# A macaron block with tree FFNs: pacing the scatters by the work beside them, and spreading the gathers of f's attention over its query steps

## The chip, the cores and the metric

The kernel runs on one core of a Trainium2 chip. Times are device microseconds (us) of that core, medians of several executions. One execution of the kernel before was also recorded by the profiler; its page and its trace are what is read here. The engines are PE (TensorE: matmuls; PEld its weight loads), DVE (VectorE), ACT (ScalarE), POOL (GpSimd) and SP (SyncE, which here only issues transfers).

## The reference

The input x has four sequences of 1024 tokens of 256 numbers, f32. Three parts are applied in turn:

```
x = x + 0.5 * ffn1(layernorm(x))
x = x + attention(layernorm(x))      # 16 heads, low-rank keys and values, rotary embedding, paged and causal
x = x + 0.5 * ffn2(layernorm(x))
```

The two ffn have the same weights. Each normalises its input to xn and then computes

```
q = tree_q(xn); k = tree_k(xn); v = tree_v(xn)         # relu
att = softmax(q k^T / sqrt(256)) v                      # within a sequence, 1024 x 1024, one head
y = xn + att
result = y + tree_f(y)                                  # gelu
```

A tree is a hard-routed feed-forward layer: each token walks down 8 levels of a binary tree, taking a side by the sign of a dot product at each node, and ends in one of 256 leaves. Each leaf is a small network of its own, 256 to 16 to 256, with biases b1 and b2.

## The kernel before, in words

**Tiles.** The 4096 tokens are 32 token tiles of 128 (NT), eight per sequence (TPB). Routing goes in groups of four tiles (GT). Leaves are taken in 32 blocks of 8, since 8 leaves of width 16 fill 128 columns. Tokens are sorted by block in DRAM, each block's share padded to whole tiles of 128 rows; there are at most 63 such leaf tiles.

**One tree.** `route` (called in groups by `routes`) transposes four tiles of xn, multiplies them with all nodes' weights (L320), compares (L328), and turns the bits into a one-hot block number per token (`oh`, L353) and running counts (`acc`, L355). `place` (L446) makes from the counts the first row of each block, and in `ranks` (L400 to L420), twice for 16 tiles each, the row (the *slot*) of each token: a 128x16 sum `sf` in f32, cast to int32 into `slot_*`. `scatter` (L529) then lets POOL issue one indirect transfer for each token tile (L531), which writes the 128 rows of that tile to their slots in DRAM (`xs`, for f `xs_f`). `leaves` (L620) loops over the leaf tiles in pipelined steps: SP loads `xg` (L629), PE transposes it (L635), DVE copies it to `xgT` (L637), PE multiplies with the block's first weights (L653, L656), DVE masks (`hm`, L661), PE transposes (L671), ACT applies the nonlinearity (L673), PE multiplies with the second weights (L678), ACT copies the result (L680) and SP writes it to DRAM, `os_q`, `os_k`, `os_v`. For f, DVE also casts each row's token number (`tok`, L666) and POOL scatters the result to token order (`ytok`, L682).

**Order within a tree FFN.** Route and place q; scatter q; route k, in whose group steps (`before(k)`) q's first weights are transposed (`load_first`, from pieces `raw_q`); q's leaves, with `place` for k running beside them, one piece per leaf tile (`with_steps`); scatter k; build k's weights and route v; k's leaves beside place for v; scatter v; build v's weights; v's leaves. During v's leaves, `coming` gathers keys and queries of the first sequence and keys of the second.

SP issues the loads ahead of this in an order that the scheduler sets: pieces of the first weights (`raw_q` and so on, L555), biases (`b_q`, L562, which `split_b1`, L568 to L575, splits into bf16 terms on DVE), second weights (`w_q`, L545) and, in the first FFN, zeros for `xs` and the sorted results (L250).

**Gathers.** `fetch` (L712) lets POOL gather a token tile's rows of q, k or v out of the sorted results (`y_q`, `y_k`, `y_v`), `fetch_b2` (L726) gathers the second biases (`b_q`, `b_k`, and for v straight into the value tile `vb`). `turned` (L933) adds the two on DVE (L938), transposes on PE (L943) and copies on ACT into `qT` or `kT` (L944); `value` (L925) adds on DVE (L931). Each of these tags has three buffers.

**The attention of q, k and v.** It is ordered by hand for PE, DVE, ACT and POOL (`in_order`): what the program writes first goes first on each engine. There are 32 steps s, one for each query tile; a sequence is also called a batch, 0 to 3. In a step `begin_weights` transposes an older tile's weights `pr` (L763) and copies them (`pT`, L764; half on DVE, half on ACT); `score` multiplies (L740), takes the maximum (`mx`, L748), scales it, and lets ACT take the exponential (L753); the older tile is then weighed with the values (L768) and `xn` updated (L770). In step 3 two more tiles are weighed. A dictionary `plan` holds what else is done: `at(step, where, do, ...)`, with where 0 (ahead of the step's scores), 1 (after the scores are issued and their maximum) or 2 (at the step's end). By the plan `begin(t)` issues the gathers of tile t's value, query and (for sequences 2 and 3) key, `add(t)` adds them, `turn(t)` does the rest. Further entries: `number` writes token numbers into xn's last column and clears `xs_f`; `begin_settling` and `settled` gather f's second bias (`b_f`) and add it and y to the residual (L1017, two adds for each tile); `place_run` places tokens for f in three runs of 24, 4 and 4 tiles (RUNS, `in_runs`), `scatter_run` scatters a run. f's routing of the last sequences lies in the same steps. The last four tiles are placed and scattered behind the attention, between pieces of the building of f's weights.

**Queues.** Transfers of SP are issued in SP's order; indirect ones in POOL's. Zeros for `xs_f` and the second weights of k, v and f go through ACT's queue. Outside the parts ordered by hand a scheduler orders the instructions; `keep_in_program_order` pins one among its like.

Of the kernel before, what the change touches and what calls it, by code (L numbers as in the profile page):

```python
# [71 lines left out]
def macaron_kernel(ctx: ExitStack, tc: tile.TileContext, a: dict, out: bass.AP):  # L72
# [327 lines left out]
    def ranks(pool, oh, acc, slot, lo, hi, first, skips=()):  # L400
# [17 lines left out]
        for part, t0 in slot:  # L418
            if t0 == lo:
                nc.vector.tensor_copy(part, sf)  # L420
# [25 lines left out]
    def place(pool, oh, acc, slot, gblk, sel):  # L446
# [6 lines left out]
        for h in range(2):  # L453
            ranks(pool, oh, acc, slot, h * NT // 2, (h + 1) * NT // 2, first)
            yield
# [8 lines left out]
    def in_runs(pool, oh, acc, slot, gblk, sel):  # L464
# [9 lines left out]
        def run(k):  # L474
# [25 lines left out]
            for t in range(lo, hi, NT // 2):  # L500
                ranks(pool, oh, acc, slot, t, min(t + NT // 2, hi), firsts[0], skips)
                yield
# [21 lines left out]
    def slot_of(slot, t):  # L524
        for part, t0 in slot:
            if t0 <= t < t0 + part.shape[1]:
                return part[:, t - t0 : t - t0 + 1]

    def scatter(f, slot, views, lo=0, hi=NT):  # L529
        for t in range(lo, hi):  # L530
            nc.gpsimd.indirect_dma_start(  # L531
                out=views[t],
                out_offset=bass.IndirectOffsetOnAxis(ap=slot_of(slot, t), axis=0),
# [4 lines left out]
    def views_of(f):  # L538
        return dram_disjoint_views(xs[f], NT)
# [168 lines left out]
    def fetch(pool, f, t, slot, bufs=3, tag=None):  # L708
# [7 lines left out]
            in_offset=bass.IndirectOffsetOnAxis(ap=slot_of(slot, t), axis=0),  # L716
# [55 lines left out]
    def ffn(first: bool, last: bool):  # L772
# [13 lines left out]
        with ExitStack() as es:  # L786
# [3 lines left out]
            for nm in FFFS:  # L790
                lows = (0, NT // 2, *RUNS[1:]) if nm == "f" else (0, NT // 2, NT)
                slot.append(
                    [
                        (idx.tile([P, hi - lo], I32, name=f"slot_{nm}{lo}"), lo)
                        for lo, hi in zip(lows, lows[1:])
                    ]
                )
# [21 lines left out]
            with ExitStack() as ws, banks(0, 8):  # L819
# [8 lines left out]
                with ExitStack() as hs, ExitStack() as rs:  # L828
                    raw = stage(rs, "raw", 1, "right")
                    pp = stage(hs, "place", 1)  # L830
                    with ExitStack() as rt:
# [43 lines left out]
                        drain(place(pp, *hot, slot[0], gblk[0], sel[0]))  # L875
                        scatter(0, slot[0], views_of(0))
                        hot = hots_of(pp, 1, 2)
                        routes(hp, 1, *hot, leaf[1], lambda k: drain(islice(build, 3 * (k > 0))))
                        drain(build)
# [5 lines left out]
                        with_steps(leaves(*what), place(pp, *hot, slot[1], gblk[1], sel[1]))  # L885
                        scatter(1, slot[1], views_of(1))
# [87 lines left out]
            with in_order(), qs, ExitStack() as ats, banks(2, 4):  # L974
# [18 lines left out]
                def begin(t):  # L993
# [8 lines left out]
                    for g in (now[0], *now):  # L1002
                        next(g)
# [569 lines left out]
```

## Time and profile before

| what | us |
|---|---|
| median of 13 executions | 2766.95 (2760.96 to 2775.38) |
| the profiled execution | 2759.72 |
| its span, first to last instruction | 2757.9 |
| PE busy | 2462.3 |
| DVE busy | 1522.4 |
| ACT busy | 1068.6 |
| POOL busy | 866.8 |

The profiled execution lies 7.2 us below the median, and 1.8 us of it lie outside the span. The mean clock granted to TensorE is 0.953 of full speed. The page shows busy times of the engines, the span in 40 slices, the chain that ended last and the costliest groups of instructions. Further views come from the trace: a timeline (start, duration, engine, line, operation, out<-in, and in brackets the idle time ahead and what ended it), a table of waits (engine, what it was about to do <- what it waited for: total, times, longest), and a table of windows (duration, then busy time and count for each engine, granted clock PEclk, share of the transfer engines, GB/s). L numbers are lines of the kernel before.

### The profile page before, as it was taken

The page shows a single profiled execution, that of the slowest core. Times are in us where ns is not written, and L with a number is a line of the kernel's source. Part 1 is how long each engine was busy: PE and PEld are TensorE (multiplying, and loading weights), DVE is VectorE, ACT ScalarE, POOL GpSimd, SP SyncE. Part 2 cuts the span into 40 slices and gives each one's busy share as a digit, 9 for nine tenths or more (in the row PEclk, how much of TensorE's full clock was granted, in tenths as well). Part 3 has the DMA queues.
Part 4 walks back from the last instruction along what each step waited for, and adds up shares of the span by engine and source line. Part 5 has one row for each costly group of instructions (what it writes and reads, how often), then busy time and mean ns, then how long its engine had stood idle before and what let it go on. Part 6 is the DMA issues. An engine that isn't in the chain of part 4 may idle for free. (4 is left out here: it accounts for less than half of the span.)

```text
span 2757.9 us, 42663 instructions
## 1 busy us (share of the span) xinstructions
PE 2462.3 (89%) x14352; PEld 1485.2 (54%) x14390; DVE 1522.4 (55%) x4105; ACT 1068.6 (39%) x2491; POOL 866.8 (31%) x978
## 2 busy tenths in 40 slices
PE   7879889899987699999999999989899899999774
PEld 3556567566665444444344344345666675666553
DVE  7654545344566566666666567556545454445643
ACT  3424334222324325555555545534343342332431
POOL 0440425356454421101101100004404255664453
PEclk9989989999998889999999999999999899999997
DMA  9965667373226400000000000005746675531455
GB/s 271 322 203 167 207 213 222 117 198 88 67 87 191 143 1 1 1 1 1 1 1 1 1 1 2 1 33 171 220 159 204 212 228 157 160 88 57 156 143 159
DMA packets 236693, 321.20 MB, mean 116 GB/s; under 512 B 28305, under 2 KB 207778, under 8 KB 232360
## 3 DMA queue, kind: packets, MB, share of 16 engines
q1 hardware_dynamic: 150480, 170.24, 20.6%
q0 software_dynamic: 38640, 100.90, 11.7%
q10 hardware_dynamic: 47336, 47.06, 5.7%
q8 instruction: 129, 2.11, 0.3%
q14 instruction: 108, 0.88, 0.1%
HBM read 193.59 MB, written 129.33 MB: 117 GB/s over the span
## 5 line engine op out<-in xcount | busy, mean ns | idle before, releaser
L1344 DVE TENSOR_REDUCE mxh<-big 128x1 f32<-128x512 f32 (+3 forms) x768 | 392.8, 551 | 220.3 <-PE big L1337 218.2
L1378 ACT ACTIVATE pTh<-big 128x512 f32<-128x512 f32 (+3 forms) x768 | 336.7, 491 | 331.9 <-PE big L1337 295.8
L1337 PE MATMUL big<-kTh,qTh 32*128 32x512 f32 (+3 forms) x1536 | 410.8, 536 | 3.2 <-ACT kTh L1319 1.6
L1371 PE MATMUL big<-qTh,kTh 32*128 32x512 f32 (+3 forms) x1536 | 351.9, 529 | 0.0
L661 DVE SCALAR_TENSOR_TENSOR hm<-eid,xg,sm 128x128 f32<-128x128 f32 x399 | 138.1, 346 | 300.7 <-PE sm L656 296.4
L673 ACT ACTIVATE hid<-sm 128x128 f32<-128x128 f32 x399 | 110.8, 278 | 425.3 <-PE sm L671 423.7
L740 PE MATMUL two<-kT,qT 128*128 128x512 f32 x512 | 236.2, 606 | 10.1 <-ACT pr L753 5.2
L768 PE MATMUL sm<-vb,pT 128*128 128x256 f32 x1024 | 234.4, 382 | 11.1 <-DVE pT L764 11.1
L320 PE MATMUL sm<-xT,nwT 128*128 128x512 f32 (+2 forms) x528 | 240.4, 599 | 2.8 <-ACT xT L314 2.8
L768 PEld LDWEIGHTS sm<-vb,pT 128*128 128x128 f32 x1024 | 191.6, 191 | 44.6 <-issue 13.4
L635 PE MATMUL sm<-ident,xg 128*128 128x128 f32 x798 | 164.6, 290 | 37.7 <-DMA xg<-xs_f 21.8
L1371 PEld LDWEIGHTS big<-qTh,kTh 32*128 32x128 f32 x1536 | 117.6, 183 | 149.2 <-DVE mxh L1344 75.8
L637 DVE COPY xgT<-sm 128x256 f32<-128x256 f32 x399 | 166.2, 416 | 27.5 <-PE sm L635 24.1
L1337 PEld LDWEIGHTS big<-kTh,qTh 32*128 32x128 f32 x1536 | 152.1, 183 | 46.0 <-ACT pTh L1378 27.4
L680 ACT COPY og<-sm 128x256 f32<-128x256 f32 x399 | 148.6, 373 | 60.5 <-PE sm L678 17.0
L1389 PE MATMUL sm<-pTh,vpad 128*32 128x512 f32 (+3 forms) x1536 | 166.7, 498 | 4.7 <-ACT pTh L1378 4.7
L328 DVE TENSOR_SCALAR bits<-sm,thr 128x512 bf16<-128x512 f32 (+1 forms) x132 | 96.5, 732 | 122.2 <-PE sm L320 121.6
L320 PEld LDWEIGHTS sm<-xT,nwT 128*128 128x128 f32 x528 | 98.5, 196 | 108.2 <-issue 89.8
L740 PEld LDWEIGHTS two<-kT,qT 128*128 128x128 f32 x512 | 94.8, 195 | 109.3 <-issue 100.9
L314 ACT COPY xT<-sm 128x512 f32<-128x512 f32 (+1 forms) x130 | 69.5, 582 | 190.4 <-PE sm L311 190.3
L531 POOL DMA_INDIRECT xs<-xn,slot_v x64 | 63.5, 993 | 240.6 <-DVE slot_v L420 221.7
L531 POOL DMA_INDIRECT xs<-xn,slot_q x64 | 61.8, 966 | 214.9 <-DVE slot_q L420 196.0
(295 smaller groups left out, 4413.2 us busy)
## 6 DMA issues: line engine op xcount, KB each, us to landing
xg<-xs SPq DMA_DIRECT2D x298, 128.5 KB
xs_f<-zero ACTq DMA_DIRECT2D x2, 8127.0 KB
xs<-zero SPq DMA_DIRECT2D x2, 8095.5 KB
xg<-xs_f SPq DMA_DIRECT2D x101, 129.0 KB
os_q<-og SPq DMA_DIRECT2D x101, 128.0 KB
os_v<-og SPq DMA_DIRECT2D x101, 128.0 KB
os_k<-og SPq DMA_DIRECT2D x96, 128.0 KB
raw_q<-in_q_w SPq DMA_DIRECT2D x8, 1024.0 KB
```

Source lines behind the costliest of these rows:

```text
L320: nc.tensor.matmul(pl, nwT[:, c, f, r * P : (r + 1) * P], xT[:, c, :], start=(c == 0), stop=(c == KC - 1),)
L635: nc.tensor.transpose(pa[:, c, :], xg[:, x0 + c * P : x0 + (c + 1) * P], ident)
L637: nc.vector.tensor_copy(xT, pa)
L661: nc.vector.scalar_tensor_tensor(hm, eid, xg[:, lf : lf + 1], ph, ALU.is_equal, ALU.mult)
L680: nc.scalar.copy(og, po)
L740: nc.tensor.matmul(ps[:, n0 : n0 + 512], qT[:, c, i * P : (i + 1) * P], kT[:, c, n0 : n0 + 512], start=(c == 0), stop=(c == KC - 1),)
L768: nc.tensor.matmul(po, pT[:, j, :], vb[:, j, :], start=(j == 0), stop=(j == TPB - 1))
L1337: nc.tensor.matmul(ps[:, :n], qT[r : r + HPAD, hg, i * P : (i + 1) * P], kT[r : r + HPAD, hg, n0 : n0 + n], start=True, stop=True,)
L1344: nc.vector.tensor_reduce(maxima(b, hg)[:, i, c, u : u + 1], ps[:, :n], AX.X, ALU.max)
L1371: nc.tensor.matmul(ps[:, off:], kT[r : r + HPAD, hg, j * P : (j + 1) * P], qT[r : r + HPAD, hg, qb * QN + off : (qb + 1) * QN], start=True ...
L1378: nc.scalar.activation(pT[:, u, off:], ps[:, off:], AF.Exp, scale=1.0 / math.sqrt(HD))
L1389: nc.tensor.matmul(acc[r : r + HPAD, off:], vpads[b % 2][:, j, 4 * hg + 2 * pair + u, :], pTs[pair][:, u, off:], start=(j == 0), stop=(j = ...
```

## The change

Four things are changed.

- `ranks` no longer casts its slots; it hands the f32 columns out in a list `rows`. Each scatter of a token tile has its own cast of one column (128x1) on DVE directly ahead of its transfer. `slot_*` is one tile per tree.
- q's scatter, 32 transfers in a row before, runs beside k's routing, five tiles for each of its group steps. k's and v's scatters run beside the leaf tiles, one token tile for each, behind the pieces of `place`. f's first run is scattered in nine places of steps 27 to 29, two or three tiles each.
- In the attention stage the gathers for q are begun for tile t at step t-6, added and turned at t-5; those of v and k of sequences 2 and 3 one tile per step. For the values of sequence 1 there are lists of steps. Settling for f takes one tile per step from step 9 on.
- `xs_f` is cleared by eight transfers in steps 6 to 20 in place of one in step 5.

```diff
...
-    def ranks(pool, oh, acc, slot, lo, hi, first, skips=()):
+    def ranks(pool, oh, acc, rows, lo, hi, first, skips=()):
...
         nc.vector.tensor_reduce(sf, row, AX.X, ALU.add)
-        for part, t0 in slot:
-            if t0 == lo:
-                nc.vector.tensor_copy(part, sf)
+        rows += [sf[:, k : k + 1] for k in range(n)]
...
-    def place(pool, oh, acc, slot, gblk, sel):
+    def place(pool, oh, acc, rows, gblk, sel):
...
         for h in range(2):
-            ranks(pool, oh, acc, slot, h * NT // 2, (h + 1) * NT // 2, first)
+            ranks(pool, oh, acc, rows, h * NT // 2, (h + 1) * NT // 2, first)
...
-    def in_runs(pool, oh, acc, slot, gblk, sel):
+    def in_runs(pool, oh, acc, rows, gblk, sel):
...
             for t in range(lo, hi, NT // 2):
-                ranks(pool, oh, acc, slot, t, min(t + NT // 2, hi), firsts[0], skips)
+                ranks(pool, oh, acc, rows, t, min(t + NT // 2, hi), firsts[0], skips)
...
-    def slot_of(slot, t):
-        for part, t0 in slot:
-            if t0 <= t < t0 + part.shape[1]:
-                return part[:, t - t0 : t - t0 + 1]
...
-    def scatter(f, slot, views, lo=0, hi=NT):
-        for t in range(lo, hi):
+    def scatter(f, slot, rows, views, *ts, pinned=True):
...
+        for t in ts:
+            cast = nc.vector.tensor_copy(slot[:, t : t + 1], rows[t])
+            if pinned:
+                tc.keep_in_program_order(cast)
...
                 out=views[t],
-                out_offset=bass.IndirectOffsetOnAxis(ap=slot_of(slot, t), axis=0),
+                out_offset=bass.IndirectOffsetOnAxis(ap=slot[:, t : t + 1], axis=0),
...
-    def views_of(f):
-        return dram_disjoint_views(xs[f], NT)
+    def scattering(f, slot, rows, n):
...
+        views = dram_disjoint_views(xs[f], NT)
+        for t in range(0, NT, n):
+            scatter(f, slot, rows, views, *range(t, min(t + n, NT)))
+            yield
...
             in_=osrt[f],
-            in_offset=bass.IndirectOffsetOnAxis(ap=slot_of(slot, t), axis=0),
+            in_offset=bass.IndirectOffsetOnAxis(ap=slot[:, t : t + 1], axis=0),
...
             for nm in FFFS:
-                lows = (0, NT // 2, *RUNS[1:]) if nm == "f" else (0, NT // 2, NT)
-                slot.append(
-                    [
-                        (idx.tile([P, hi - lo], I32, name=f"slot_{nm}{lo}"), lo)
-                        for lo, hi in zip(lows, lows[1:])
-                    ]
-                )
+                slot.append(idx.tile([P, NT], I32, name=f"slot_{nm}"))
...
                         build = load_first(raw, 0, w1, ahead)
-                        drain(place(pp, *hot, slot[0], gblk[0], sel[0]))
-                        scatter(0, slot[0], views_of(0))
+                        rows = []
+                        drain(place(pp, *hot, rows, gblk[0], sel[0]))
+                        going = scattering(0, slot[0], rows, 5)
                         hot = hots_of(pp, 1, 2)
-                        routes(hp, 1, *hot, leaf[1], lambda k: drain(islice(build, 3 * (k > 0))))
-                        drain(build)
...
+                        def beside(k):
+                            drain(islice(build, 3 * (k > 0)), islice(going, 1))
...
+                        routes(hp, 1, *hot, leaf[1], beside)
+                        drain(build, going)
...
                         b1, ahead = load_raw(raw, 1)
-                        with_steps(leaves(*what), place(pp, *hot, slot[1], gblk[1], sel[1]))
-                        scatter(1, slot[1], views_of(1))
+                        rows = []
+                        with_steps(
+                            leaves(*what),
+                            place(pp, *hot, rows, gblk[1], sel[1]),
+                            scattering(1, slot[1], rows, 1),
+                        )
...
                     ahead += [load_part(raw2, 2, *p) for p in PART[2:]]
-                    with_steps(leaves(*what), place(pp, *hot, slot[2], gblk[2], sel[2]))
-                    scatter(2, slot[2], views_of(2))
+                    rows = []
+                    with_steps(
+                        leaves(*what),
+                        place(pp, *hot, rows, gblk[2], sel[2]),
+                        scattering(2, slot[2], rows, 1),
+                    )
...
                 vbs.append(ap.tile([P, TPB, E], F32, name="vb1", bufs=1))
-                views = views_of(3)
-                placing = in_runs(pf, *hot_f, slot[3], gblk[3], sel[3])
+                views = dram_disjoint_views(xs[3], NT)
+                rows_f = []
+                placing = in_runs(pf, *hot_f, rows_f, gblk[3], sel[3])
...
-                def begin(t):
...
+                def begin(kinds, t):
...
                     m, n = b % 2, slice(i * P, (i + 1) * P)
-                    now = [value(vbs[m], t, i), turned(ap, 0, t, qTs[m][:, :, n])]
-                    if b > 1:
-                        now.append(turned(ap, 1, t, kTs[m][:, :, n]))
-                    coming_in[t] = now
-                    for g in (now[0], *now):
+                    for kind in kinds:
+                        if kind == "v":
+                            g = value(vbs[m], t, i)
+                            next(g)
+                        else:
+                            to = (qTs, kTs)[kind == "k"][m]
+                            g = turned(ap, int(kind == "k"), t, to[:, :, n])
...
-                def add(t):
-                    for g in coming_in[t]:
-                        next(g, None)
...
-                def turn(t):
-                    drain(*coming_in.pop(t))
+                        coming_in[kind, t] = g
...
+                def add(kinds, t):
+                    for kind in kinds:
+                        next(coming_in[kind, t], None)
...
+                def turn(kinds, t):
+                    for kind in kinds:
+                        drain(coming_in.pop((kind, t)))
...
-                def scatter_run(k):
-                    scatter(3, slot[3], views, RUNS[k], RUNS[k + 1])
+                def go(*ts):
+                    scatter(3, slot[3], rows_f, views, *ts, pinned=False)
...
-                    clear(nc.scalar, xs[3])
...
-                for do, steps in (
-                    (add, ((4, 0), (4, 0), (4, 2), (5, 0), (5, 0), (6, 0), (7, 0), (7, 0))),
-                    (turn, ((4, 1), (4, 1), (5, 0), (5, 1), (5, 1), (6, 1), (7, 1), (7, 1))),
-                    (begin, ((1, 2), (2, 2), (3, 1), (4, 1), (4, 1), (5, 0), (5, 1), (5, 1))),
-                ):
-                    for i, (step, where) in enumerate(steps):
-                        at(step, where, do, TPB + i)
+                def clear_some(k):
...
+                    clear(nc.scalar, xs[3][k * 8 * P : min((k + 1) * 8 * P, NSLOT)])
...
+                for t in range(TPB, NT):
+                    at(t - 6, 1, begin, "q", t)
+                    at(t - 5, 0, add, "q", t)
+                    at(t - 5, 1, turn, "q", t)
+                for i in range(TPB):
+                    t = TPB + i
+                    at((1, 1, 1, 2, 2, 3, 3, 4)[i], 2, begin, "v", t)
+                    at((2, 3, 3, 4, 4, 5, 5, 6)[i], 0, turn, "v", t)
                 for b in range(1, B - 1):
-                    for do, steps in (
-                        (add, ((2, 0), (3, 0), (4, 0), (5, 0), (5, 0), (6, 0), (7, 0), (7, 1))),
-                        (turn, ((2, 1), (3, 1), (4, 1), (5, 1), (5, 1), (6, 1), (7, 1), (7, 2))),
-                        (begin, ((0, 2), (0, 2), (0, 2), (2, 1), (3, 1), (4, 1), (5, 1), (5, 1))),
-                    ):
-                        for i, (step, where) in enumerate(steps):
-                            at(b * TPB + step, where, do, (b + 1) * TPB + i)
+                    for i in range(TPB):
+                        n, t = b * TPB + max(0, i - 1), (b + 1) * TPB + i
+                        at(n, 2, begin, "vk", t)
+                        at(n + 1, 1 if i else 0, add, "vk", t)
+                        at(n + 1, 2 if i else 1, turn, "vk", t)
                 at(5, 2, number)
+                for k in range(8):
+                    at(6 + 2 * k, 0, clear_some, k)
+                for t in range(15):
+                    at(t + 9, 2, begin_settling, "f", t)
+                    at(t + 10, 2, settled, t)
+                at(24, 2, begin_settling, "ffk", 15, 16, 17)
+                at(25, 2, settled, 15, 16, 17)
+                at(25, 2, begin_settling, "ff", 18, 19)
+                at(26, 2, settled, 18, 19)
                 at(26, 2, place_run, 0, 1)
-                at(27, 0, begin_settling, "qkqk", *range(20, 24))
+                at(27, 0, begin_settling, "kkkf", *range(20, 24))
                 at(27, 0, place_run, 0, 2)
-                at(27, 0, scatter_run, 0)
+                at(28, 2, settled, *range(20, 24))
+                for step in range(27, 30):
+                    t = 8 * (step - 27)
+                    for where, ts in enumerate((range(t, t + 2), range(t + 2, t + 5), range(t + 5, t + 8))):
+                        at(step, where, go, *ts)
...
                 at(30, 2, place_run, 1, 2)
-                at(30, 2, scatter_run, 1)
-                for step, ts in (
-                    (15, range(4)), (23, range(4, 8)), (24, range(8, 12)), (25, range(12, 16)),
-                    (26, range(16, 20)), (27, range(20, 24)),
-                ):
-                    at(step + 1, 2, settled, *ts)
-                    if step < 27:
-                        at(step, 2, begin_settling, "ffqk", *ts)
+                at(30, 2, go, *range(RUNS[1], RUNS[2]))
...
                     place_run(2, 1)
-                    scatter_run(2)
+                    go(*range(RUNS[2], NT))
...
                     place_run(2, 9)
```

## The prediction

> **What bounds the kernel now.** First the page: engine sums, and the slices beneath them.
>
> ```profile
> PE 2462.3 (89%) x14352; PEld 1485.2 (54%) x14390; DVE 1522.4 (55%) x4105; ACT 1068.6 (39%) x2491; POOL 866.8 (31%) x978
> ...
> PE   7879889899987699999999999989899899999774
> ...
> POOL 0440425356454421101101100004404255664453
> ```
>
> TensorE (PE) is the bound nearly everywhere, so only what opens or closes its gaps counts. Then the table by stage, for both tree FFNs' attention stages and the loading stretch before the first leaves.
>
> ```profile
> core 0: us, PE busy (x) PEld busy (x) DVE busy (x) ACT busy (x) POOL busy (x), PEclk, DMA share, GB/s
> 88.00:141.30 53.30, 43.39 (x225) 24.99 (x227) 27.13 (x77) 20.60 (x33) 30.94 (x32) 0.92 1.03 338
> ...
> 503.70:830.00 326.30, 309.94 (x1346) 208.60 (x1354) 162.93 (x400) 90.34 (x173) 182.21 (x188) 0.98 0.39 115
> 2280.60:2597.00 316.40, 302.44 (x1308) 203.30 (x1316) 159.50 (x389) 88.28 (x167) 182.13 (x188) 0.99 0.38 112
> 519.90:526.40 6.50, 6.46 (x10) 2.83 (x11) 3.16 (x6) 1.68 (x3) 4.98 (x6) 0.57 0.34 91
> ```
>
> In the attention stages PE idles 16.4 of 326.3 us and 14.0 of 316.4: evener gathers can win no more than that. 88 to 141 is bound by transfers (share 1.03). The last row is for the clock, below. The waits of the first attention stage, PE alone, say what its idle time is:
>
> ```profile
> PE sm L768 <- DVE pT L764: 5.5, 4, 2.0
> PE two L740 <- ACT pr L753: 4.6, 2, 3.9
> PE sm L395 <- DVE acc_f L355: 2.9, 2, 1.5
> PE sm L943 <- DVE y_q L938: 1.7, 3, 0.8
> ```
>
> Only L943, the turning of gathered queries, and part of L768 belong to the gathers. Now the start of the second FFN's attention, where the change regroups most; GpSimd (POOL) first, then VectorE (DVE), then PE.
>
> ```profile
> 2294.42 0.95 POOL L712 DMA_INDIRECT y_v<-os_v,slot_v  x1 [0.30 <-issue]
> 2295.68 0.95 POOL L726 DMA_INDIRECT vb<-in_v_b,leaf_v  x1 [0.31 <-issue]
> 2296.93 0.95 POOL L712 DMA_INDIRECT y_v<-os_v,slot_v  x1 [0.30 <-DVE mx L749]
> 2298.18 0.95 POOL L712 DMA_INDIRECT y_q<-os_q,slot_q  x1 [0.30 <-issue]
> ```
>
> ```profile
> 2295.23 1.22 DVE L748 TENSOR_REDUCE mx<-two 128x1 f32<-128x1024 f32 x1
> ...
> 2296.56 0.42 DVE L931 TENSOR_TENSOR vb<-vb,y_v 128x256 f32<-128x256 f32 x1
> 2297.20 0.43 DVE L931 TENSOR_TENSOR vb<-vb,y_v 128x256 f32<-128x256 f32 x1 [0.22 <-DMA y_v<-os_v,slot_v]
> ```
>
> ```profile
> 2295.84 3.60 PE L740 MATMUL two<-kT,qT 128*128 128x512 f32 x8
> 2299.27 1.04 PE L763 MATMUL sm<-ident,pr 128*128 128x128 f32 x8
> 2300.14 3.62 PE L768 MATMUL sm<-vb,pT 128*128 128x256 f32 x16
> ...
> 2315.69 0.60 PE L943 MATMUL sm<-ident,y_q 128*128 128x128 f32 x4
> ```
>
> To be seen: a gather costs POOL 1.255 us start to start; its row is added 2.78 us after its issue (2294.42 to 2297.20); the values of batch 0 arrive just in time; PE runs without a gap from 2294.96 on, and turns tile 8's query only at 2315.69, when it lies ready.
>
> **The change, part by part.**
>
> *Tile 8's gathers (the main term).* Before, query 8 is begun at (1,2), added at (4,0), turned at (4,1). After, it is begun at (2,1), added at (3,0), turned at (3,1), and POOL's order ahead of it becomes: last values of batch 0, vb8, y_v8, vb9, y_v9, vb10, y_v10, y_q8, b_q8. DVE's order adds value 8 at (2,0), ahead of mx of step 2, where before the maximum came first. The y_v buffers are three, so y_v9 must wait until value 6 is added, which stands behind that mx. PE's order puts the four turns of y_q8 straight behind step 3's scores, ahead of two query tiles' weighing (L763, L768).
>
> Second FFN: y_v8 issued 2296.93 (row) + 2.78 = 2299.7, added 2300.1; mx 1.22 and its scaling 0.15; value 6 added by 2301.9; y_v9 0.27 later, 2302.1; then four more issues of 1.255, b_q8 at 2307.15; + 2.78 = 2309.9; added 0.42 and seen by PE at 2310.5. PE is through with step 3's scores at 2299.4 (2295.84 + 3.60). Stall 11.1 us, nothing else in PE's order to cover it; the weighing queued behind it waits too. First FFN: y_v8 issued at 523.19, added 526.0 to 526.4, mx 527.6, value 6 528.1, y_v9 528.4, b_q8 533.4, landed 536.2, PE 536.75, free since 526.4: 10.35 us. Without any wait for the buffer b_q8 would land 2.6 us sooner, stall about 8: the lower bound. Upper bound: one of the two landings as long as 4.17 us, DVE's longest wait for a y_v in the first stage (at 515.64), +1.4.
>
> *The clock after the stall.* In the first FFN 3.91 us without matmuls (516.03 to 519.94) were followed by eight score matmuls in 6.45 us instead of the 3.60 of the row above, at a granted clock of 0.57: +2.85. In the second FFN 4.08 us idle cost +2.96 in the same way. I add 2.85 and 2.95; bounds 0 and twice as much, as no row shows the clock after 10 us.
>
> [...] The row shows 6.5 us of low clock, and I go by it.
>
> *Later gathers.* Begun a step and more ahead: query 9 lands near 2317.6 and is needed near 2327.6, no stall. At the starts of batches 2 and 3 key 17's add comes at 595.8 against PE at 595.4: 0.5 each, +1 per FFN. POOL's load, 7 gathers x 1.255 = 8.8 us a step, stands against a mean step of 9.6 us.
>
> *Gaps that go.* The waits at L943 (1.7), and pT copies behind eight settling adds in a block: 0.43 + 0.82 + 0.38 + 0.98 = 2.6 us in the first FFN, 0.43 + 0.86 + 0.55 + 1.05 = 2.9 in the second. Bounds 0 and all.
>
> *Step 27.* Before, eight L1017 adds (766.99 to 770.30) hold the pT copy until 770.22 and PE waits 1.96 us. After, only four stand ahead: -1.6; two or three scatter casts take +0.5: -1.1 per FFN.
>
> *Casts.* 32 casts of 128x1 for each scatter replace one per part. Nearest row: tok's cast of the same shape, 147 ns. In the leaf loop it lies between xgT and hm, where DVE idles 0.86 us per leaf tile; f's leaves, which have such a cast today, run at 1.60 us per tile against 1.55. Cost 0 to 0.05 x 64 = 3 us per FFN; taken 0, cover: DVE's idle time.
>
> *Paced scatters.* An issue takes 0.963 + 0.305 us on POOL, 32 of them 40.6 us; one per 1.55 us leaf tile ends k's and v's scatter 10 to 14 us later (213 for 199.8, 361 for 348), while the first reads of xs for k are at 295 and of v's later: hidden, 0. Leaf tiles run 1.55 us apart inside and outside today's burst, so nothing is won there either: bound 0 to -2.
>
> *q's scatter and the loads before the first leaves.* In the second FFN casts and blocks come first, the scatter ends 1.4 us later and the first xg with it: +1.4. In the first FFN b_v's loads move ahead of raw_q's fourth part on SP's queue and wait for DVE's split of b_k, near 106: raw_q's last part is issued at about 107.5 instead of 91.7, w_q, os_q's zeros and raw_k behind it. The queue is bound by bytes, so I take 3.4 us of that as lost; against it DVE no longer waits 7.74 us for b_v at 143.65, which held PE at L395 for 6.07 us. Net -1; bounds -6 (that gap gone, nothing late) and +16 (the late issue carried through).
>
> *xs_f's zeros.* Eight issues of 0.39 us on ACT instead of one, in a stage where ACT is busy 28%: 0.
>
> *End.* Four casts for one: within 0.2.
>
> **Sum.** First FFN 10.35 + 2.85 - 2.6 - 1.1 + 1 - 1 = +9.5; second 11.1 + 2.95 - 2.9 - 1.1 + 1 + 1.4 = +12.45. Together +22. The profiled execution took 2759.72 us (span 2757.9 and 1.8 around it), 7.2 under the median; so 2781.7 against it, and 2766.95 + 22 = 2789 for the median.
>
> **The rivals.**
>
> *A. Pacing frees transfers (faster).* One mechanism: scatters no longer burst against the leaf tiles' loads, and PE's waits at L635 for xg<-xs (15.8 us, and 13.4 for its weight loads) go. It decides above 22 us; all 29.2 gone gives 2760. For: the transfers' share is 1.03 at 88 to 141. Against: leaf tiles keep their pace inside the burst, and those waits lie at the leaves' starts. Chance 0.09.
>
> *B. The late raw_q part carries through.* +16 instead of -1 at the first FFN's head: 2806. For: SP's queue is in order and w_q stands behind. Against: bytes bound it, and the order of transfers changes little else. 0.12.
>
> *C. POOL too full.* 8.8 of 9.6 us with steps as short as 8.0: if each of 16 steps per FFN waits 0.5 to 1 us for a gather, +16 to +32: 2805 to 2821. Against: buffers let POOL run ahead. 0.09.
>
> *D. No stall.* If the order on the engines lets query 8 land in time, -2.6 - 2.9 - 2.2 + 2.4 (batch starts and second head) - 1 + 2 remain: -4, 2763, and with small losses none: 2767. Against: three buffers and POOL's order. 0.05.
>
> The main case has 0.65.
>
> **How the numbers follow.** The main case alone: low from stalls of 8 with no clock loss and the first head at -6: 8 - 2.6 - 1.1 + 1 - 6 = -0.7, 8 - 2.9 - 1.1 + 1 + 1.4 = +6.4, so 2773; high 22 + 1.4 x 2 + 5.8 (clock twice) + 3, so 2800. To leave out no more than 2 in 10 the range reaches into B and C above: 2771 to 2808. 0.2%, 5.5 us, is about what a measurement here tells from no change. Faster: A and half of D, 0.11; same: the rest of D and the main case's low edge, 0.06; slower 0.83.
>
> **What would show it.** Right: in each attention stage one PE idle stretch of 8 to 12 us ahead of the turns of y_q between step 3's scores and the next weighing, put down to the adds of y_q; y_v9's issue waiting for DVE; the clock low behind it; L943's other waits gone; eight short zero issues on ACT. Wrong: PE without a gap there (D); a first L653 well after 150 us (B); waits of PE or DVE for gathers in most steps (C); shorter spans of the leaves (A). The forecast fails most easily in the order of landing: should y_v9 not need value 6's buffer, or DVE pass mx sooner, the stall shrinks to 8.

## The result, and the profile after

The changed kernel takes 2790.71 us (median of 10 executions, 2781.35 to 2800.56); the kernel before, run beside it, 2766.44 (46 executions). The ratio is 1.0085, interval 1.0071 to 1.0100: slower by 24.3 us, where +22 was forecast. A later repetition (e11 below) gave 2778.9 against 2757.57, 1.0077 (1.0056 to 1.0097).

The profiled execution of the changed kernel took 2797.46 us (span 2795.6), 6.8 above its median, that of before 7.2 below its own. So 37.7 us lie between the two spans, some 13 more than between the medians. The stages are cut at the first score matmul and at the first transpose of f's weights behind the attention. They compare so:

| stage, us | before | after | difference |
|---|---|---|---|
| first FFN, to the first score matmul | 503.7 | 506.8 | +3.1 |
| first FFN, attention of q, k, v | 325.5 | 337.2 | +11.7 |
| f's leaves, the 16-head attention, second q, k, v | 1451.4 | 1461.7 | +10.3 |
| second FFN, attention of q, k, v | 321.9 | 333.5 | +11.6 |
| to the end | 155.4 | 156.4 | +1.0 |

The two attention stages make 23.3 us, about the whole difference of the medians. The other three rows, +14.4, hold the paced scatters of q, k and v, but also much that the change leaves alone. In the profile of the repetition the same three rows lie 6.6 us below those of before, so no cost or gain can be read from them; its two attention stages lie 7.2 and 9.7 us above. The page of the changed kernel, engine sums and PE's slices:

```profile
PE 2484.8 (89%) x14352; PEld 1502.2 (54%) x14390; DVE 1538.6 (55%) x4341; ACT 1070.9 (38%) x2491; POOL 862.1 (31%) x978
...
PE   7889889799986799999999999988999888999884
```

PE has as many instructions as before and is 22 us longer busy: slower matmuls, not more (the mean granted clock is 0.943 in this profile, 0.953 in that of before). What it waits for in the first attention stage follows. Lines have moved: L741, L764 and L769 were L740, L763 and L768, the adds of values L939 were L931, the turning of gathered queries L951 was L943, and its add L946 was L938.

```profile
PE sm L951 <- DVE y_q L946: 9.8, 1, 9.8
PE two L741 <- ACT pr L754: 3.9, 2, 3.3
PE sm L395 <- DVE acc_f L355: 2.8, 2, 1.4
PE sm L764 <- ACT pr L754: 2.4, 1, 2.4
```

One wait of 9.8 us stands where three short ones stood. Its place in the second FFN, on POOL, DVE and PE:

```profile
2322.12 0.95 POOL L713 DMA_INDIRECT y_v<-os_v,slot_v  x1 [0.30 <-issue]
2323.37 0.95 POOL L727 DMA_INDIRECT vb<-in_v_b,leaf_v  x1 [0.30 <-issue]
2325.64 0.94 POOL L713 DMA_INDIRECT y_v<-os_v,slot_v  x1 [1.33 <-DVE vb L939]
...
2330.64 0.95 POOL L727 DMA_INDIRECT b_q<-in_q_b,leaf_q  x1 [0.30 <-issue]
```

```profile
2324.94 0.42 DVE L939 TENSOR_TENSOR vb<-vb,y_v 128x256 f32<-128x256 f32 x1 [5.20 <-DMA y_v<-os_v,slot_v]
2325.29 1.22 DVE L749 TENSOR_REDUCE mx<-two 128x1 f32<-128x1024 f32 x1
2326.54 0.15 DVE L750 TENSOR_SCALAR mx<-mx 128x1 f32<-128x1 f32 x1
2326.61 0.75 DVE L939 TENSOR_TENSOR vb<-vb,y_v 128x256 f32<-128x256 f32 x2
...
2333.45 0.42 DVE L946 TENSOR_TENSOR y_q<-y_q,b_q 128x256 f32<-128x256 f32 x1 [5.49 <-issue]
```

```profile
2320.38 3.60 PE L741 MATMUL two<-kT,qT 128*128 128x512 f32 x8
2333.93 0.69 PE L951 MATMUL sm<-ident,y_q 128*128 128x128 f32 x2 [9.95 <-DVE y_q L946]
2334.42 1.91 PE L764 MATMUL sm<-ident,pr 128*128 128x128 f32 x8
2336.12 4.59 PE L769 MATMUL sm<-vb,pT 128*128 128x256 f32 x16
```

This is the forecast chain but for one link. Value 8 is added at 2324.94 after DVE has waited 5.20 us for it, and the maximum follows, values 6 and 7 only then. The gather of y_v9 waits 1.33 us on POOL, but not for value 6: it is issued at 2325.64, 0.27 us behind the end of value 8's add and before value 6 is added at 2326.61. b_q of tile 8 is issued at 2330.64 and the query added at 2333.45. PE has had nothing since 2323.98. Behind it the matmuls are slow. The windows of the changed kernel (duration, busy time of each engine, clock, transfers) right behind the stall, and after that:

```profile
core 0: us, PE busy (x) PEld busy (x) DVE busy (x) ACT busy (x) POOL busy (x), PEclk, DMA share, GB/s
...
537.50:544.60 7.10, 7.10 (x26) 6.22 (x27) 2.67 (x6) 2.05 (x4) 5.27 (x7) 0.64 0.33 98
544.60:549.80 5.20, 5.20 (x33) 4.71 (x32) 1.87 (x5) 0.58 (x1) 1.53 (x2) 1.00 0.29 79
...
2333.93:2340.60 6.67, 6.67 (x27) 5.95 (x28) 2.67 (x6) 2.05 (x4) 4.92 (x6) 0.69 0.37 106
```

How far the changed kernel lies behind before at the start of each step's scores, counted from the first score matmul, in the first and the second FFN:

| step | 3 | 4 | 8 | 10 | 27 | 28 | 30 | end |
|---|---|---|---|---|---|---|---|---|
| first, us | -0.6 | 11.0 | 7.8 | 9.5 | 9.6 | 7.4 | 10.8 | 11.7 |
| second, us | -0.5 | 11.9 | 8.5 | 10.0 | 9.5 | 7.1 | 10.7 | 11.6 |

The loss comes in one step, step 3. From step 4 to 8 the kernel makes up some 3 us, but part of that is work put off: by step 8 it has turned five gathered tiles, the kernel before eight, and a turn takes PE some 0.4 us (0.38 for its two matmuls in e7). By step 10 it has turned nine against eight, and 1.5 to 1.7 us are gone again. Step 27 wins over 2, and from step 28 on over 4 are given back.

### The profile page after: what moved, and what is told of

The parts are those of the page before. It is cut to its first block, busy times and chain, and to the rows that moved or that the text cites. A ratio compares the mean times of both kernels' runs of the same rounds, so it can differ in the third digit from the quotient of the medians.

```text
span 2795.6 us, 43155 instructions
## 1 busy us (share of the span) xinstructions
PE 2484.8 (89%) x14352; PEld 1502.2 (54%) x14390; DVE 1538.6 (55%) x4341; ACT 1070.9 (38%) x2491; POOL 862.1 (31%) x978
## 3 DMA queue, kind: packets, MB, share of 16 engines
q0 software_dynamic: 38640, 100.90, 11.9%
## 5 line engine op out<-in xcount | busy, mean ns | idle before, releaser
L741 PE MATMUL two<-kT,qT 128*128 128x512 f32 x512 | 237.8, 609 | 9.1 <-ACT pr L754 4.6
L769 PE MATMUL sm<-vb,pT 128*128 128x256 f32 x1024 | 237.9, 386 | 5.8 <-DVE slot_f L525 4.0
L769 PEld LDWEIGHTS sm<-vb,pT 128*128 128x128 f32 x1024 | 194.5, 194 | 35.3 <-issue 5.4
L638 DVE COPY xgT<-sm 128x256 f32<-128x256 f32 x399 | 166.2, 417 | 28.4 <-PE sm L636 26.9
L681 ACT COPY og<-sm 128x256 f32<-128x256 f32 x399 | 148.5, 372 | 62.9 <-PE sm L679 20.9
L328 DVE TENSOR_SCALAR bits<-sm,thr 128x512 bf16<-128x512 f32 (+1 forms) x132 | 96.5, 733 | 109.5 <-PE sm L320 109.0
L741 PEld LDWEIGHTS two<-kT,qT 128*128 128x128 f32 x512 | 95.4, 196 | 109.2 <-issue 101.6
L749 DVE TENSOR_REDUCE mx<-two 128x1 f32<-128x1024 f32 x64 | 78.2, 1223 | 113.0 <-PE two L741 112.8
```

The costliest lines, as they stand in the source:

```text
L638: nc.vector.tensor_copy(xT, pa)
L681: nc.scalar.copy(og, po)
L741: nc.tensor.matmul(ps[:, n0 : n0 + 512], qT[:, c, i * P : (i + 1) * P], kT[:, c, n0 : n0 + 512], start=(c == 0), stop=(c == KC - 1),)
L769: nc.tensor.matmul(po, pT[:, j, :], vb[:, j, :], start=(j == 0), stop=(j == TPB - 1))
```

## The experiments

The theory was the stall ahead of y_q8's turns with the low clock behind it. Against it stood: the paced scatters and their casts are what costs; and POOL is too full, so that the wait only moves. Each kernel was timed beside the kernel before on its chip. The ratios are to that.

**Query 8 one step later (e1).** Of the changed kernel, only:

```diff
-                    at(t - 5, 0, add, "q", t)
-                    at(t - 5, 1, turn, "q", t)
+                    late = int(t == TPB)
+                    at(t - 5 + late, 0, add, "q", t)
+                    at(t - 5 + late, 1, turn, "q", t)
```

> Only the query of token tile 8 is added and turned one step later (at step 4 instead of 3); all else is the changed kernel. Theory 1, the stall ahead of y_q8's turns with the low clock behind it (9.82 and 9.95 us idle, and 2.7 and 2.2 us of slower matmuls in the changed kernel's profile): both go, about -24, some 2767, no PE gap above 1 us between step 3's scores and the next weighing. Theory 2, the paced scatters and their casts are what costs: within 3 us of the changed kernel, 2790. Theory 3, POOL is too full with seven gathers a step: the wait moves to another gather, 2780 to 2790.

Measured 2769.85, before 2764.54: 1.0024 (1.0012 to 1.0036). The wait for y_q is gone from PE's list, and most of the loss with it, so the scatters are cleared as its main cause. Not all went: at step 4 the run still lies 4.0 and 5.8 us behind before. DVE and PE of its second FFN tell why:

```profile
2310.33 0.43 DVE L939 TENSOR_TENSOR vb<-vb,y_v 128x256 f32<-128x256 f32 x1 [5.26 <-DMA y_v<-os_v,slot_v]
2310.67 1.22 DVE L749 TENSOR_REDUCE mx<-two 128x1 f32<-128x1024 f32 x1
...
2312.66 0.68 DVE L765 COPY pT<-sm 128x512 f32<-128x512 f32 x1
```

```profile
2308.70 1.04 PE L764 MATMUL sm<-ident,pr 128*128 128x128 f32 x8
2313.39 6.54 PE L769 MATMUL sm<-vb,pT 128*128 128x256 f32 x16 [3.66 <-DVE pT L765]
```

DVE's wait for value 8 holds not only the maximum but also the pT copy behind it; PE's weighing waits 3.66 us for that and then runs at 6.54 us instead of 3.62. In the changed kernel this second wait was hidden under the longer one.

**Value 8 later, query as changed (e2).**

```diff
-                    at((2, 3, 3, 4, 4, 5, 5, 6)[i], 0, turn, "v", t)
+                    at((2, 3, 3, 4, 4, 5, 5, 6)[i], 0 if i else 2, turn, "v", t)
```

> Only the value of token tile 8 is added at the end of step 2, behind values 6 and 7, instead of ahead of that step's maximum; y_q8 keeps its place. The prediction's chain (value 8 ahead of the maximum, value 6 behind it, buffer of y_v9) says that y_v9 is issued without a wait and b_q8 lands 1.3 to 2.6 us sooner per FFN: stall 7.3 to 8.6 us instead of 9.9, 2785 to 2788. If the buffer were the whole cause, the stall would go and the time would be 2767. If POOL's order alone sets it, no change: 2790.

Measured 2784.26: 1.0069 (1.0050 to 1.0088). POOL and PE of the second FFN:

```profile
2314.60 0.95 POOL L713 DMA_INDIRECT y_q<-os_q,slot_q  x1 [0.30 <-issue]
2315.85 0.94 POOL L727 DMA_INDIRECT b_q<-in_q_b,leaf_q  x1 [0.30 <-issue]
```

```profile
2319.14 0.69 PE L951 MATMUL sm<-ident,y_q 128*128 128x128 f32 x2 [9.76 <-DVE y_q L946]
```

POOL now issues without a wait for a buffer, and yet the stall is 9.76 us, 8.50 in the first FFN. That makes 18.3 us over both where the changed kernel had 19.8, not 7.3 to 8.6 each as expected. The repetition of the changed kernel (e11), which does wait for the buffer, has 8.31 and 9.47, and the intervals of the two ratios overlap. So the buffer was a small link, worth at most the 1.33 us that POOL had waited. The long one is the place of y_q8 in POOL's order, behind eight values and three more.

**Query 8 first on POOL (e3).**

```diff
-                    at(t - 6, 1, begin, "q", t)
+                    if t == TPB:
+                        at(1, 2, begin, "q", t)
+                    else:
+                        at(t - 6, 1, begin, "q", t)
```

> Only the gathers of tile 8's query are begun ahead of those of values 8, 9 and 10 on POOL (at the end of step 1); it is added and turned in step 3 as in the changed kernel. If it is the place in POOL's order that makes the query late, b_q8 is issued at least five gathers of 1.26 us earlier and lands some 8 to 9 us sooner: stall 0 to 2 us, 2767 to 2772. Theory 2: 2790. If DVE's waits for values 9 and 10 in step 3 hold the rest: up to 2775.

Measured 2777.67: 1.0041 (1.0024 to 1.0058); better by half, not by all, above the range expected. DVE and PE:

```profile
2315.45 0.42 DVE L939 TENSOR_TENSOR vb<-vb,y_v 128x256 f32<-128x256 f32 x1 [7.35 <-DMA y_v<-os_v,slot_v]
...
2318.39 0.41 DVE L946 TENSOR_TENSOR y_q<-y_q,b_q 128x256 f32<-128x256 f32 x1
```

```profile
2318.85 0.69 PE L951 MATMUL sm<-ident,y_q 128*128 128x128 f32 x2 [6.44 <-DVE y_q L946]
```

The query lies ready, but its add stands on DVE behind value 8's, which came 2.5 us later for it: DVE waits 7.35 us there, PE 6.44. So two early adds each hold the path, and taking one away leaves the other.

**The gathers' plan alone, put into the kernel before (e4).** begin, add and turn and their lists from the change; scatters, settling and zeros of before.

> The kernel before with only the plan of begin, add and turn from the changed kernel; scatters, settling and zeros stay as before. Theory 1: +20 to +25 over before, about 2789, with both stalls of 10 us. Theory 2: within 3 us of before, 2767.

Measured 2791.62 against 2764.54: 1.0096 (1.0077 to 1.0115), +27 us. The gathers alone make all of the loss (the interval overlaps that of the changed kernel); at step 4 it lies 10.6 and 11.9 us behind, as the changed kernel does.

**Values and query later (e6, e9, e12).** Of the changed kernel, with e1's edit:

```diff
-                    at((1, 1, 1, 2, 2, 3, 3, 4)[i], 2, begin, "v", t)
-                    at((2, 3, 3, 4, 4, 5, 5, 6)[i], 0, turn, "v", t)
+                    at((2, 2, 3, 3, 4, 4, 5, 5)[i], 2, begin, "v", t)
+                    at((4, 4, 5, 5, 6, 6, 7, 7)[i], 0, turn, "v", t)
```

> The kernel of e6 and e9 a third time, now beside the changed kernel on one chip. Where before takes about 2766: 2758 to 2763 if the values' adds ahead of step 2's maximum were the rest of the loss, else 2765 to 2770. Where before takes about 3155: 2970 to 2985, 10 to 20 us under the changed kernel.

Beside it on the same chip the changed kernel itself (e11):

> The changed kernel itself, unaltered. On a chip where before takes about 2766: 2787 to 2795 as in the first result. On a chip where before takes about 3155 because DVE and ACT stop while POOL issues gathers or scatters one behind the other: the run with matmuls in the stall gave 2994 there, the scatters alone 2980; I expect 2985 to 2998, 0.948 of before. If the two stalls at step 3 cost more there, since gathers land later, above 3000.

Measured: before 2757.57, changed 2778.9, with values and query later 2758.04, 0.9996 of before (0.9980 to 1.0012). The edit wins 20.9 us; in the two profiles the attention stages differ by 8.7 and 13.2, together 21.9. PE in the first FFN, behind step 3's scores, has no gap left:

```profile
517.89 1.04 PE L764 MATMUL sm<-ident,pr 128*128 128x128 f32 x8
518.76 3.62 PE L769 MATMUL sm<-vb,pT 128*128 128x256 f32 x16
522.22 1.04 PE L764 MATMUL sm<-ident,pr 128*128 128x128 f32 x8
523.09 3.62 PE L769 MATMUL sm<-vb,pT 128*128 128x256 f32 x16
```

So the early place of value 8 and query 8 explains the loss. The edit moves the gathers of the values behind query 8's on POOL as well as the adds on DVE, and it does not tell the two apart; e1 and e3 do so for the query. On this chip before is 9 us faster than in the first result, and the changed kernel's 2778.9, expected at 2787 to 2795, moved with it. The expectation of 2758 to 2763 was written for a before of 2766, that is 3 to 8 us less. Measured is a difference of 0 (interval -5.5 to +3.3), so the rest of the change is worth 5.5 us at most here; in the profiles the attention stages of e12 are 1.5 and 3.5 us shorter than those of before.

**Another behaviour, on two other chips.** The next four kernels and two repetitions fell on two chips on which the kernel before takes 3157 and 3153 us instead of 2757 to 2766. These two are called the second kind below, the others the first. The verdicts of these runs hold for such a chip.

Values and query later were timed there first (e6, e9):

> The changed kernel with the values of tiles 8 to 15 begun one step later and added from step 4 on (two per step), and query 8 added and turned in step 4; nothing stands ahead of step 2's maximum. The run with the query alone later lost its y_q wait but kept 4.0 and 5.8 us at step 4, where DVE waited for value 8 ahead of step 2's maximum and of a pT copy. If that is the second half of the cause, these go as well: about -10 from that run's 2770, some 2760, below before; PE's gaps from step 2 to 4 as in the kernel before. If the POOL queue itself is too slow with this order, a gap of 2 us or more remains: 2765 to 2770.

> The kernel of e6 once more. There the kernel before took 3157 us on its chip, and DVE and ACT stopped for up to 16 us at a time for something that none of the kernel's own queues shows. On a chip where before takes about 2766 and these stops are missing: 2758 to 2763 if the values' adds ahead of step 2's maximum were the rest of the loss, 2765 to 2770 if POOL's order keeps a gap. On a chip with the stops: 0.94 of before again.

Measured 2981.5 against 3156.79, 0.9429 (0.9400 to 0.9458), and 2974.04 against 3152.54, 0.9434.

The scatters alone (e5 and e10): the kernel before with the change's `ranks`, `scatter`, `scattering` and f's `go`, everything else of before.

> The kernel before with only the scatters of the change (own casts, q's beside k's routing, k's and v's one per leaf tile, f's over steps 27 to 29); gathers, settling and zeros as before. The prediction's terms for this part: -1 and +1.4 at the heads, 0 in the leaves, up to +1 at step 27: 2764 to 2769 where before is 2766. Theory 2 (casts on DVE delay the leaf tiles' first matmuls, whose weight loads wait for slot_k and slot_v in the changed kernel): +3 to +10.

> The kernel of e5 once more. On a chip where before takes about 2766: 2764 to 2769 by the prediction's terms (heads -1 and +1.4, step 27 up to +1, leaves 0); 2769 to 2776 if the casts delay the leaf tiles. On a chip with the stops: 0.94 of before again.

Measured 2981.41, 0.9434 (0.9405 to 0.9462), and 2979.04, 0.9462: there the pacing of the scatters alone wins about 175 us. Their worth on a chip of the first kind was not measured alone; e12 less before bounds it, together with all else but the early adds. The same holds for settling and zeros, next.

Settling and zeros alone (e8): the kernel before with the change's settling entries and its `clear_some`.

> The kernel before with only the settling of f one tile per step and xs_f's zeros in eight parts on ACT's queue. The prediction: settling wins 1.1 to 2.5 per FFN at the pT copies behind blocks of adds, the zeros cost 0: 2761 to 2765 where before is 2766. If eight parts of zeros disturb the gathers (each step's gather would land later and PE wait), 2768 to 2775.

Measured 3133.3 against 3156.79, 0.9916 (0.9886 to 0.9945). This run still scatters in bursts, and so it is the one to lay beside e5. DVE's waits in e8, then in e5 (what it was about to do, what it waited for: total, times, longest); "remote" stands for something that the profile does not name:

```profile
DVE hm L661 <- remote: 135.2, 18, 16.4
DVE xn L770 <- remote: 103.0, 10, 16.1
```

```profile
DVE hm L662 <- remote: 19.1, 5, 5.8
DVE xn L771 <- remote: 128.1, 12, 16.0
```

In the profiles from the other chips no such wait is listed. Two of these stops in e8, in q's leaves, and POOL beside them:

```profile
201.46 0.35 DVE L661 SCALAR_TENSOR_TENSOR hm<-eid,xg,sm 128x128 f32<-128x128 f32 x1 [9.91 <-remote]
...
221.05 0.35 DVE L661 SCALAR_TENSOR_TENSOR hm<-eid,xg,sm 128x128 f32<-128x128 f32 x1 [14.98 <-remote]
```

```profile
215.00 0.96 POOL L531 DMA_INDIRECT xs<-xn,slot_k  x1 [0.30 <-issue]
216.27 0.96 POOL L531 DMA_INDIRECT xs<-xn,slot_k  x1 [0.30 <-issue]
```

While POOL issues k's 32 scatters in a row from 176.0 to 217.2, DVE stops for 9.9 and 15.0 us and goes on 4 us after the last. From the first leaf of q to the first of k e8 takes 178.0 us and e5 147.9, from k's to v's 142.8 and 109.5; in the second FFN 193.5 and 160.2, 142.8 and 107.6. With the heads, from q's first weight piece to its first leaf (89.0 and 78.9, 87.4 and 77.6) this is 151.8 of the 157.0 us between the two spans. In the attention stages, where POOL gathers (in e5 one behind the other from 625.1 to 642.3 us, with a stop of DVE of 16.05 that ends at 645.63), both have the stops still: 408.5 and 399.8 us in e5, 400.2 and 399.8 in e8, against 325.5 and 321.9 of before on the first kind of chip. What the stops wait for stays open.

**Matmuls in the stall (e7).** The changed kernel with

```diff
+                def fill():
+                    spare = sm([P, 512])
+                    for _ in range(20):
+                        nc.tensor.matmul(spare, ident, kTs[0][:, 0, :512], start=True, stop=True)
+
+                at(3, 1, fill)
```

> The changed kernel with 20 matmuls of 128x512 (9 us at full clock) put between step 3's scores and the turns of y_q8, in both FFNs; nobody reads their results. If the slow matmuls behind the stall come from PE's idle time, they run at full clock now: weighing as fast as later ones (3.62 us for 16), -2.2 to -2.7 per FFN, 2784 to 2787, though PE does more work. If the clock is set by something else, the weighing stays at 4.6 to 5.1 us and the time at 2790.

It fell on a chip of the second kind, so its time (2993.55, 0.9465 of before there) can't be set against 2790; the changed kernel without the fill was not run there. And the fill was twice as long as meant: 20 f32 matmuls are 40 in the record and take 17.33 us. The question of the clock is answered all the same. PE in the second FFN:

```profile
2438.18 17.33 PE L1062 MATMUL sm<-kT,ident 128*128 128x512 f32 x40
2455.35 0.38 PE L951 MATMUL sm<-ident,y_q 128*128 128x128 f32 x2
2455.57 1.04 PE L764 MATMUL sm<-ident,pr 128*128 128x128 f32 x8
2456.44 3.62 PE L769 MATMUL sm<-vb,pT 128*128 128x256 f32 x16
```

Without idle time ahead, the same transposes take 1.04 us instead of 1.91 and the weighing 3.62 instead of 4.59. So with the idle time filled, the slow matmuls behind it are gone.

## Why the prediction was right

The forecast was 2789, the result 2790.71. The main case came true, and by its mechanism: e1 took the query's wait away, e12 the rest, e4 made the loss without any of the other parts. That the sum came so close is partly luck, as the terms show.

*Tile 8's stall.* Forecast 10.35 and 11.1 us, measured 9.82 and 9.95 (8.31 and 9.47 in e11). One link of the chain was wrong: y_v9 did not wait for value 6, behind the maximum, but only for value 8. So POOL lost 1.26 and 1.33 us there, not the 2.6 of the text; the 1.3 us between are about what the second FFN's stall came out shorter. (In e2, with values 6 and 7 added ahead of 8, y_v9 did not wait for value 8 either; it seems to take the buffer that is emptied first.) The working also missed that the pT copy stands behind value 8 as well, a second stall hidden under the first. So rival D, no stall by a query in time alone, would not have reached before: e1 is the proof. (D's sum is also off: the terms of the main sum without stall and clock make -5.3, not -4.)

*The clock behind it.* Forecast 2.85 and 2.95. Measured against the full-speed rows, 2.66 in the first FFN (turns +0.31, transposes +0.87, weighing +1.48) and 2.15 in the second (+0.31, +0.87, +0.97). In e1 a gap of 3.66 us cost 2.9. In the first FFN the earlier gap had also shrunk, from 3.91 to 3.29 us, and its score matmuls from 6.45 to 5.28, which was not forecast: -1.8. In e11 they take 6.67 again, so this varies between executions of one kernel.

The losses behind the stalls of step 3, between 3.05 and 9.95 us long in the changed kernel, e1 to e4 and e11, lie between 1.6 and 2.9 us. Gaps of 2.01 and 2.37 us were followed by slow matmuls too (below). The row of 0.57, behind a gap of 3.91 us, sized the stall's term, 0.2 and 0.8 us too high.

*Later gathers and gaps that go.* PE's three waits ahead of the turns (1.7 and 1.9 us) and its wait in step 17 (1.0 and 1.1) went as forecast. In their place stand small ones, 1.8 and 1.1 us together, none longer than 0.73 and none put down to a gather's add. From step 4 to step 27 the kernel makes up 1.4 and 2.4 us, 0.4 of each because tile 8's turn was done a step earlier; the terms made 1.6 and 1.9.

*Step 27 and behind.* Step 27 won 2.3 and 2.4 instead of 1.1: PE's wait of 1.96 us for the pT copy went whole. In the first FFN the slow weighing behind it (5.38 us for 16 matmuls) went too, but the next wait grew from 0.86 to 2.37 us. From step 28 on 4.4 and 4.5 us were lost where next to nothing had been put. PE in steps 28 and 29 of the first FFN, changed kernel:

```profile
787.62 1.24 PE L764 MATMUL sm<-ident,pr 128*128 128x128 f32 x8 [2.37 <-ACT pr L754]
788.65 5.19 PE L741 MATMUL two<-kT,qT 128*128 128x512 f32 x8
...
804.49 5.38 PE L769 MATMUL sm<-vb,pT 128*128 128x256 f32 x16 [2.01 <-DVE slot_f L525]
```

Gaps stood there before as well, of 0.86 and 1.83 us, in the second FFN of 2.55 and 1.83, and their matmuls ran at 3.60 and 3.69 us. Now both gaps of both FFNs are followed by matmuls that take 1.6 to 1.7 us longer, at a granted clock of 0.72 and 0.68 instead of 1.00. The length does not decide it. Step 27 of before, in the first FFN and in the second:

```profile
771.05 5.38 PE L768 MATMUL sm<-vb,pT 128*128 128x256 f32 x16 [1.96 <-DVE pT L764]
...
2544.39 3.69 PE L768 MATMUL sm<-vb,pT 128*128 128x256 f32 x16 [1.96 <-DVE pT L764]
```

Nor does the kernel alone: in e11, the changed kernel again, the gaps are 2.38 and 2.00 us; in its first FFN neither is followed by slow matmuls, in its second one. The stretch from step 28 on costs 1.1 us with none (e11), 2.8 with one (e11, e12) and 4.4 to 4.5 with both. Of the 24 such gaps in the profiles of the changed kernel, e1 to e3, e11 and e12, 15 were followed by slow matmuls, of the eight at the same places in before and e4 one. Why some are and others are not stays open. This was the term of the sum that was mis-sized most: the working counted gaps of 2 us by their length, and the clock only behind the two long ones.

*The sum.* The attention stages together: forecast 10.5 and 11.05, measured 11.7 and 11.6. Stall and clock came out at 12.5 and 12.1 where 13.2 and 14.05 had been put; the slow matmuls from step 28 on, 3.3 and 3.4 us in no term, made up for it. This is the luck in the number.

*Heads.* The second FFN's, from q's first weight piece to its first leaf: forecast +1.4, measured 57.7 to 58.9, and 58.6 to 59.4 in the other runs with the new scatters, against 57.6 in e4 with the old. For the first FFN's the sum took -1, though its own figures, 3.4 lost and 6.07 won, make -2.7. It can't be judged: 71.3 and 70.5 us with the old scatters (before, e4), 64.5 to 71.3 with the new, 67.6 to 67.8 on the chip of e4 (e1 to e3).

*Casts and paced scatters, taken as 0.* The leaf loops of q and k in e12 (148.7 and 105.6; 157.1 and 105.8) are within 1.2 us of before (148.7 and 105.6; 155.9 and 105.3). That held. Rival B did not come: the first leaf is no later. Rival C did not come on this kind of chip: behind step 3 no wait of PE is put down to a gather's add.

*Rival A* is the one to look at again. On the first kind of chip it did not come: PE's waits for xg at L635, 15.8 us before, are 13.0 after and 12.2 in e4 with the old scatters. On the second kind pacing won not 29 us but about 175, though by stops of DVE and ACT that go and not by the waits that A named, and it turns the sign: even the changed kernel with 17 us of unused matmuls in each FFN is 0.9465 of before there. Nothing in the profile of before could show it, since that profile came from a chip without these stops.

## What to carry to other kernels

In a program ordered by hand, an add of gathered data put one step early holds everything behind it on its engine (in the second FFN here 5.20 us on DVE for value 8, 9.95 on PE for query 8). Follow the gather from its place in the issuing queue to its landing before it is moved: here 1.255 us for each transfer ahead of it and 2.8 for its landing decided. Where one wait is removed, look for the next on the same engine (value 8 behind query 8). A gap of 2 us on TensorE cost nearly as much again here in slow matmuls behind some (5.38 us for 16 behind 2.01) and next to nothing behind others (3.69 behind 1.96). And time a change that reshapes bursts of indirect transfers on more than one chip: the paced scatters won about 175 us on two of these, and on one of the others the change without the early adds at most 5.5.

## What the runs showed of the hardware that was not expected

Two of the chips run the same kernel before in 3153 to 3157 us, the others in 2757 to 2766. On the former DVE and ACT stop for something that the profile does not name (in e8, DVE for up to 28.4 us ahead of a copy of q's weights, 18 times and for 16.4 at most at the masks, ACT for up to 18.4). Those in q's leaves of e8 and in the attention of e5 fall where POOL issues indirect transfers one behind the other (176.0 to 217.2 us and 625.1 to 642.3), and the longest of DVE's there, 14.98 and 16.05 us, end 3 to 4 us behind the last. With the scatters spaced at a leaf tile's pace, 1.55 us instead of 1.27, DVE's stops at the masks make 19.1 us in e5 against 135.2 in e8 (q's leaf loop 147.9 us against 178.0). POOL's issue itself takes 0.96 us on both.

The granted clock fell behind some gaps of 2 us and not behind others of the same length: behind one gap of 1.96 us 16 weighing matmuls take 5.38 us at a granted clock of 0.68, behind another 3.69 at 1.00.
